# Costs in a list scheduler: durations by which the instructions of a transformer block are ordered, set to those of its trace

## The chip, the cores and the metric

The kernel runs on one core of a Trainium2 chip, in one launch. The metric is the device time of that launch in microseconds (us), as the median of several executions. The core's engines each work through an instruction list of their own: TensorE (PE, matrix products), VectorE (DVE), ScalarE (ACT), GpSimd (POOL) and SyncE (SP, which here only issues DMA transfers). Semaphores hold an instruction back until what it needs is there. The order inside each list is fixed when the program is built.

## The reference

One transformer block over an input x of 4 sequences of 1024 rows of 512 fp32 numbers. `c` makes six vectors per sequence; attention has 16 heads of 32 with one shared key and value head; the feed-forward part has Walsh-Hadamard transforms (`fwht`) before each of its two products (gate and up count as one). In the code below, cut and shortened, the first half is attention with its causal softmax and output projection, `gb` is clamped like `ga`, and `t` is the feed-forward part.

```python
mod = (_silu(c) @ wmod).reshape(4, 6, 1, -1)
sa, ca, ga, sb, cb, gb = (mod[:, n] for n in range(6))
ga = (2 * (ga >= 0) - 1) * jnp.maximum(jnp.abs(ga), 0.25)
h = _layernorm(x) * (1 + ca) + sa
x = x + ga * attention(h)
h = _layernorm(x) * (1 + cb) + sb
t = fwht(h * SU_ug) / 64
t = _silu(t @ W_gate.T * (Wscale_g * 64)) * (t @ W_up.T * (Wscale_u * 64))
t = fwht(t * SU_dp) / 64
x = x + gb * (t @ W_down.T * (Wscale_dp * 64))
```

## The kernel before

**Work.** The 4096 rows are 8 blocks of 512 rows, each of 4 tiles of 128 rows. A block goes through attention, tile by tile, and then through the feed-forward part (FFN) as a whole. The second transform and the scales are multiplied into the down weights once, in a preparation at the start (`butterflies` L965, `transforms` L986 and L989, copied by ACT at L992 and stored as wd_d). `mods` (L882, L886, L891, L932) makes the six vectors.

**Attention of a tile.** Score products (L503, PE), row minima of the negated scores (L527, DVE), exponentials with their sums (L550, ACT), reciprocals (L564, DVE), scaling (L584, ACT), transposes (L599, DVE), the product with the values (L627, PE, many small 32x32 products) and its copy out (L641, ACT). For the first block, products with a folding matrix (L684) and a copy (L687, ACT) bring the heads together; for the others an exchange through memory (o_d) and two additions on POOL (L664, L665). The output projection is called at L300, and its result is multiplied by `ga` on DVE (L701). POOL adds it to the residual (L716, L718), the sum is stored (x_d<-xr), and DVE makes its statistics (L305, L306), POOL the reciprocal deviation (`rstd_op`, L311 and L312).

**From attention to the FFN.** In the first three blocks DVE normalises (L316), PE transposes (L339), and products with a Hadamard matrix (L796), a copy (L801, ACT) and sums (L804, DVE) give the FFN's input `bt`. From the fourth block on (block 3, counted from 0) the generator `transformed` does it outside PE: two DVE operations normalise and modulate (L747, L749), 18 additions and subtractions of 256 columns on POOL make the transform (L755), DVE transposes in 32x32 squares (L758), four stores take a tile to memory (xTf_d<-xr) and two loads bring back half a block (bt<-xTf_d). In both forms four DVE subtractions (L808) then form T1 to T4.

**FFN.** The gate and up products of one of 16 chunks are one 2x2 product in Strassen's form, with seven products instead of eight (`gate_up`, all at L1078). POOL makes the four sums of weights (`mixes`, L1042), ACT copies partial results out (`copies`, L1152 and L1156), DVE adds them (`sums`, L1165), and `multiply` forms silu(gate) × up: tanh on ACT (L1181), a product for both halves of the rows (L1183, DVE), then g1 for the second half (L1186) and g0 for the first (L1191). `down` (L1216, PE) takes the first half of the rows while the chunks come, the second half later, with down weights in a ring of three buffers, loaded again for each half (wd<-wd_d). `outputs` multiplies by `gb` (L1245) and adds the residual (L1250). All transfers that SyncE issues stand at L289, in one order.

**What orders the work.** Nothing of this order is written by hand. Every step is a Python generator (a stream) that yields operations `Op(eng, cost, emit, reads, writes)`. `Flow` is a list scheduler that runs while the program is built. It keeps the time at which each engine becomes free and at which each buffer was written and read, by the operations' costs and not by the chip; for every stream's next operation it works out when that could begin, takes the earliest and all others of the same engine that begin within SLACK (0.3) of it, and emits the one of the lowest rank. Ranks stand in a list at the end of the kernel. The engines' lists are the order of emission. A result from another engine counts as there LATENCY (0.2) after its end; a change of PE's mode costs SWITCH (0.16); a transfer costs 3.9 per MB on one shared channel, and 1.5 to land. So a cost changes no instruction; it moves the point at which an operation is taken, and what is taken before it.

```python
some = [h for h in heads if h[2][2].eng == lead[2].eng and h[0] <= first + self.SLACK]
return min(some, key=lambda h: (h[2][0](), h[0]))
```

FFN weights are loaded and FFN products emitted only after a hand-over (stream `hand_over`), which waits for the preparation's last transform and `mods`.

Of the kernel before, what the change touches and what calls it, by code (L numbers as in the profile page):

```python
# [11 lines left out]
ALU = mybir.AluOpType  # L12
# [15 lines left out]
HB = 256  # L28
# [18 lines left out]
class Flow:  # L47
# [4 lines left out]
    LATENCY = 0.2  # L52
    SLACK = 0.3
    SWITCH = 0.16
    TRANSFER = 3.9

    def __init__(self):
# [10 lines left out]
    def ready(self, op):  # L68

        t = 0.0  # L70

        def after(found):
            if found is None:
                return 0.0
            at, eng = found
            return at if eng == op.eng else at + self.LATENCY

        for k in op.reads:
            if k not in self.wrote:
                return None  # L80
            t = max(t, after(self.wrote[k]))
        for k in op.writes:
            t = max(t, after(self.wrote.get(k)), after(self.read.get(k)))
        return t
# [76 lines left out]
def adaln_block(ctx, tc, x_d, small_d, const_d, wmod_d, qwT_d, kwT_d, vwT_d, vb_d, owT_d, ob_d,  # L161
# [147 lines left out]
    def rstd_op(dst, src, keys, key):  # L309
        def emit():  # L310
            nc.gpsimd.tensor_scalar_add(dst, src, EPS)  # L311
            nc.gpsimd.tensor_tensor(dst, dst, mhalf[:, 0:dst.shape[-1]], ALU.pow)  # L312
        return Op("POOL", 2.0, emit, keys, [key])

    def norm_op(x, xk, m, rs, rkey):
        return Op("DVE", 0.62, lambda: nc.vector.tensor_scalar(x, x, m, rs, ALU.subtract, ALU.mult), [rkey], [xk])  # L316
# [290 lines left out]
    def attend():  # L607


        while True:  # L610
            yield until(to_attend, "turns")
            if not to_attend:
                break
            u = to_attend.popleft()
            yield banks.have(4)
            bb = banks.take(4)
            w = u.heads * 32
            nkt = u.kmax // P
            pv = u.head(0, u.heads).rearrange("p (h k) -> p h k", k=u.kmax)

            def products():
                for kt in range(nkt):
                    v0 = u.kv[kt // NT] * (TB // 32) + kt % NT * 4
                    for g in range(4):
                        for c in range(4):
                            k = kt * P + 32 * c
                            nc.tensor.matmul(ps[rows[c], bb[g], 0:w], vrep[rows[g], v0 + c, :],  # L627
                                             pv[rows[g], :, k:k + 32],
                                             start=(kt == 0), stop=(kt == nkt - 1))
            yield Op("PE", nkt * (mm(w) + 0.22), products,  # L630
                     [u.key(h) for h in range(u.heads)] + [("vrep", j) for kb in range(u.t + 1) for j in u.half_keys(
                         kb, TB if kb < u.t else u.kmax - kb * TB)],
                     [bk(b) for b in bb] + [("through", u.k)], mode="tiles")
            st.attended += 1
            for h0 in range(0, u.heads, 8):
                half = (u.h0 + h0) // 8
                qn = 2 * (u.i * NT + u.ql) + half
                yield lambda: st.folded >= qn - 1
                o = oT[:, half].rearrange("p j (c g q) -> p g c j q", c=2, g=4)
                for g in range(4):  # L640
                    yield Op("ACT", act_cost(HB), lambda: nc.scalar.copy(  # L641
                        o[:, g], ps[:, bb[g], h0 * 32:h0 * 32 + HB].rearrange("p (c j q) -> p c j q", c=2, q=32)),
                        [bk(bb[g])], [("oT", half)])
                    if h0 + 8 == u.heads:
                        banks.give(bb[g])
                (to_finish if u.i < EXCHANGED else to_exchange).append((u.i, u.ql, half))
            if u.h0 + u.heads == H and u.ql == NT - 1:
                st.attended_blocks = u.i + 1
        over["attend"] = True

    def exchange():


        while True:
            yield until(to_exchange, "attend")
            if not to_exchange:
                break
            i, ql, half = to_exchange.popleft()
            o, key = oT[:, half], ("oT", half)
            yield load(0.5, o_d[half], o, [("o_d", half)], [key])  # L660
            for j, r in enumerate(rows):
                yield load(0.125, o[r], o_d[half].rearrange("(c d) j x -> j d c x", c=4)[j], [key], [("o_d", half)])
            o = o.rearrange("p c x -> p (c x)")
            yield Op("POOL", 1.3, lambda: nc.gpsimd.tensor_add(o[:, 0:512], o[:, 0:512], o[:, 512:1024]), [], [key])  # L664
            yield Op("POOL", 0.66, lambda: nc.gpsimd.tensor_add(  # L665
                aT[:, 2 * half:2 * half + 2, :].rearrange("p c q -> p (c q)"), o[:, 0:HB], o[:, HB:512]), [key], ["aT"])
            st.folded += 1
            to_finish.append((i, ql, half))
        over["exchange"] = True

    def finish():

        while True:
# [4 lines left out]
            if i < EXCHANGED:  # L678
                yield banks.have(1)
                bo, = banks.take(1)  # L680

                def folds():
                    for j, r in enumerate(rows):
                        nc.tensor.matmul(ps[r, bo, 0:HB], fold, oT[:, half, j, :], start=True, stop=True)  # L684
                yield Op("PE", 0.5, folds, [("oT", half)], [bk(bo)], mode="cols")
                st.folded += 1
                yield Op("ACT", act_cost(HB), lambda: nc.scalar.copy(  # L687
                    aT[:, 2 * half:2 * half + 2, :], ps[:, bo, 0:HB].rearrange("p (c q) -> p c q", c=2)), [bk(bo)], ["aT"])
                banks.give(bo)
            if half == 0:  # L690
# [42 lines left out]
    def transformed():  # L733


        for n in range(ROWS * NT, NBLK * NT):
# [3 lines left out]
            if n == ROWS * NT or n % NT == 0 and new_batch(i):  # L740
                yield lambda: st.normed >= ROWS
                for k, (dst, c) in enumerate(((sc2r, 0), (bi2r, 2))):
# [1 line left out]
                               [("gates", 3 + k)])  # L744
            yield lambda: bool(to_fwht)
            _, m, rs = to_fwht.popleft()
            yield Op("DVE", 0.7, lambda: nc.vector.scalar_tensor_tensor(x, x, m[:, 0:1], sc2r, ALU.subtract, ALU.mult),  # L747
                     [("v4", 0), ("mvf", j)], [xk])
            yield Op("DVE", 0.7, lambda: nc.vector.scalar_tensor_tensor(x, x, rs, bi2r, ALU.mult, ALU.add),  # L749
                     [("v4", 2), ("rstdf", j)], [xk])  # L750
            u, w = x, ht
            for _ in range(9):
# [9 lines left out]
    def second_norms():  # L762


        for i in range(NBLK):
            b = order[i][0]
            for hf in range(2):
# [30 lines left out]
                yield Op("PE", mm(HB, 4), products, [("v4", dc) for dc in range(NDC)] + ["had"],  # L798
                         [bk(b) for b in bb], mode="full")
                w2 = u2.rearrange("p a n -> p (a n)")  # L800
                yield Op("ACT", act_cost(512), lambda: nc.scalar.copy(w2, ps[:, bb[1], :]), [bk(bb[1])], ["u2"])  # L801
                banks.give(bb[1])
                for e, k in (("add", hf), ("sub", 2 + hf)):
                    yield Op("DVE", 0.7, lambda: getattr(nc.vector, "tensor_" + e)(  # L804
                        bt[:, k].rearrange("p a n -> p (a n)"), ps[:, bb[0], :], w2), [bk(bb[0]), "u2"], [("bt", k)])
                banks.give(bb[0])
            for o, u, w in ((T1, B12, B11), (T2, B22, T1), (T3, B22, B12), (T4, B21, T2)):
                yield Op("DVE", 0.7, lambda: nc.vector.tensor_sub(bt[:, o], bt[:, u], bt[:, w]),  # L808
                         [("bt", u), ("bt", w)], [("bt", o)])
            st.normed = i + 1  # L810

# [59 lines left out]
    def mods():  # L871
        for _ in range(6):
# [10 lines left out]
            yield Op("PE", mm(512), products, [("raw", s)], [bk(o)], mode="cols")  # L883
            busy[s] = False
            m = ym
            yield Op("ACT", act_cost(512), lambda: nc.scalar.copy(m, ps[:, o, :]), [bk(o)], ["ym"])  # L886
            pm = ps[:, o, 0:NDC * B].rearrange("p (a b) -> p a b", b=B)

            def summed():
# [145 lines left out]
    def mixes():  # L1035
        yield lambda: st.prepared
        for k in range(NW):
            a = weights(k)
            yield lambda: st.wg_loaded > k and st.wu_loaded > k and st.sums_used > k - 2
            for e, o, x, y in (("add", "S1", "A21", "A22"), ("sub", "S2", "S1", "A11"), ("sub", "S4", "A12", "S2"),  # L1040
                               ("sub", "S3", "A11", "A21")):
                yield Op("POOL", 0.66, lambda: getattr(nc.gpsimd, "tensor_" + e)(a[o][0], a[x][0], a[y][0]),  # L1042
                         [a[n][1] for n in (x, y) if n != "A21" or o != "S3"], [a[o][1]])
            st.mixed = k + 1

# [98 lines left out]
    def copies():  # L1144
        for n in range(2 * NW):
# [3 lines left out]
            bank = where[k]  # L1149
            if kind == "sp":  # L1150
                yield lambda: st.g1mul > k - 2
                yield Op("ACT", act_cost(512), lambda: nc.scalar.copy(  # L1152
                    s[:, 0:3:2, :], ps[:, bank, :].rearrange("p (a n) -> p a n", a=2)), [bk(bank)], [sk[0], sk[2]])
                st.sp = k + 1
            else:
                yield Op("ACT", act_cost(HB), lambda: nc.scalar.copy(s[:, 1, :], ps[:, bank, 0:HB]), [bk(bank)], [sk[1]])  # L1156
                to_sum.append(("g1", k))

    def sums():
# [15 lines left out]
    def multiply():  # L1175
        for k in range(NW):
# [3 lines left out]
            th, bank = ff["th"], where[k]  # L1180
            yield Op("ACT", act_cost(512), lambda: nc.scalar.activation(  # L1181
                th, s[:, 0:2, :], AF.Tanh, scale=wgh[:, f:f + 1]), [sk[0], sk[1]], ["th"])
            yield Op("DVE", 0.7, lambda: nc.vector.scalar_tensor_tensor(  # L1183
                th, th, 1.0, s[:, 0:2, :], ALU.add, ALU.mult), [sk[0], sk[1]], ["th"])
            yield lambda: st.v > k and st.downs1 > k - NFC
            yield Op("DVE", 0.46, lambda: nc.vector.scalar_tensor_tensor(  # L1186
                ff["g1"][:, f, :], th[:, 1, :], cg[:, f:f + 1], s[:, 2, :], ALU.mult, ALU.mult),
                [sk[2], "th"], [("g1", f)])
            st.g1mul = k + 1
# [128 lines left out]
```

## Time and profile before

| What | Before |
|---|---|
| Median of 3 executions (lowest, highest) | 2051.14 us (2047.05, 2052.68) |
| Profiled execution: its own time | 2046.4 us |
| Span in the profile | 2044.6 us |
| Mean granted TensorE clock | 0.989 |
| DMA traffic | 285.47 MB, mean 140 GB/s |
| L747, L749 (DVE), mean | 0.93, 0.95 us (0.75 where undisturbed) |
| L1183, L1186, L1191 (DVE), mean | 0.80, 0.66, 0.47 us |
| L808 (DVE), mean | 0.77 us |
| L1152, L1156 (ACT), mean | 0.59, 0.37 us |
| L641, L687 (ACT), mean | 0.38, 0.37 us |
| L801, L886 (ACT), mean | 0.59, 0.58 us |
| L1042 (POOL), mean of its four | 0.83, 0.77, 0.76, 0.75 us |
| L665 (POOL), mean | 0.77 us |
| L311 and L312 together (POOL), mean | 0.96 us (tile of the second norm) |
| L755 (POOL), mean | 0.64 us |

The profile shows one execution. "Busy" is the time in which an engine has an instruction under way; a row such as `L1078 PE MATMUL ps<-bt,wg` names line, engine, operation and tiles (written first). An idle time before an instruction is put down to what ended last before it ("<-DVE bt L808"), or to "issue" where the profile shows no such thing. Slices divide the span into 40 equal parts, and a digit gives tenths; PEclk is the TensorE clock that was granted, in tenths of full speed. The waits of an engine are listed with their total in us, their number and the longest.

### The profile page before, as it was taken

The numbers are of one execution on the slowest core, as the hardware profiler recorded it, in microseconds if no ns is written. First come the engines' busy times: TensorE is split into PE (matmuls) and PEld (weight loads), VectorE is DVE, ScalarE is ACT, GpSimd is POOL, SyncE is SP. The second block draws the span as 40 slices with busy tenths as digits, with TensorE's granted clock in tenths as the row PEclk, the third lists the DMA queues.
The fourth block names the chain that finished last, engine by engine and source line by source line (L and its number), as shares of the span: only waits on it lengthen the run. The fifth ranks groups of instructions, "written<-read, shape, count | busy, mean of one in ns | idle before, by whom it ended". The sixth has DMA issues, their size and how long they took to land.

```text
span 2044.6 us, 41680 instructions
## 1 busy us (share of the span) xinstructions
PE 1955.1 (96%) x15720; PEld 1264.7 (62%) x15720; DVE 1376.8 (67%) x3131; ACT 1133.5 (55%) x2391; POOL 973.5 (48%) x1246
## 2 busy tenths in 40 slices
PE   6997999999999999999999999998999999999998
PEld 4554666646676566655576566664566746675774
DVE  3885867777747567787748787766578877732441
ACT  3676766676557455666546665577356765510220
POOL 2662454414433576554545156534775535653441
PEclk9897999999999999999999999999999999999999
DMA  6424544454335755465344553357544355335333
GB/s 213 120 73 128 154 149 129 155 168 126 103 111 163 204 145 140 138 183 157 113 115 116 186 160 104 98 147 196 182 129 130 102 170 143 113 112 175 116 104 116
DMA packets 368464, 285.47 MB, mean 140 GB/s; under 512 B 112500, under 2 KB 300020, under 8 KB 368264
## 3 DMA queue, kind: packets, MB, share of 16 engines
q1 hardware_dynamic: 364328, 280.39, 47.0%
q10 hardware_dynamic: 3936, 2.43, 0.4%
q8 instruction: 124, 2.03, 0.4%
q14 instruction: 76, 0.62, 0.1%
HBM read 220.83 MB, written 61.91 MB: 138 GB/s over the span
## 4 chain that ended last, share of the span: by engine, by line
PE 85%; DVE 5%; DMA 5%; issue 2%; POOL 2%; SPq 1%; ACT 0%; POOLq 0%; ACTq 0%; DVEq 0%
PE ps L1078 36%; PE ps L1216 19%; PE ps L300 11%; PE ps L627 9%; PE ps L503 7%; DMA wd<-wd_d 1%; DMA raw<-in_wmod 1%; SPq L289 1%; DVE p L599 1%; DVE p L527 1%; PE ps L986 1%; PE ps L989 1%; DMA x_d<-xr 1%; DVE s L1165 1%; DVE g L1191 0%
## 5 line engine op out<-in xcount | busy, mean ns | idle before, releaser
L1216 PE MATMUL ps<-wd,g 128*128 128x512 f32 x1024 | 482.3, 605 | 27.4 <-DVE g L1191 16.7
L550 ACT ACTIVATE p<-p,nm 128x512 f32<-128x512 f32 (+7 forms) x512 | 391.2, 767 | 62.4 <-DVE nm L527 62.3
L1078 PE MATMUL ps<-bt,ws 128*128 128x256 f32 x1536 | 378.3, 382 | 2.8 <-DVE bt L808 1.9
L584 ACT ACTIVATE p<-p,rden 128x640 f32<-128x640 f32 (+7 forms) x480 | 348.0, 783 | 48.5 <-DVE rden L564 48.4
L599 DVE STREAM_TRANSPOSE p<-p 128x512 f32<-128x512 f32 (+7 forms) x256 | 342.7, 1358 | 42.3 <-ACT p L584 38.7
L1165 DVE TENSOR_TENSOR s<-ps,s 128x256 f32<-128x256 f32 x384 | 160.2, 420 | 298.1 <-PE ps L1078 227.5
L1216 PEld LDWEIGHTS ps<-wd,g 128*128 128x128 f32 x1024 | 185.6, 190 | 258.4 <-issue 189.9
L1078 PEld LDWEIGHTS ps<-bt,ws 128*128 128x128 f32 x1536 | 289.6, 191 | 58.8 <-issue 13.6
L527 DVE CUSTOM_DVE_ANT_0 p<-ps,maskw 128x512 f32<-128x512 f32 (+3 forms) x512 | 278.4, 583 | 69.2 <-PE ps L503 68.5
L1042 POOL TENSOR_TENSOR ws<-wu 128x256 f32<-128x256 f32 x128 | 105.8, 827 | 365.6 <-DMA wu<-in_wupT 309.2
L1078 PE MATMUL ps<-bt,wu 128*128 128x256 f32 x1024 | 269.0, 385 | 0.0
L1078 PE MATMUL ps<-bt,wg 128*128 128x256 f32 x1024 | 250.9, 381 | 0.4 <-DVE g L1191 0.3
L1078 PEld LDWEIGHTS ps<-bt,wu 128*128 128x128 f32 x1024 | 189.6, 190 | 83.0 <-issue 39.0
L1078 PEld LDWEIGHTS ps<-bt,wg 128*128 128x128 f32 x1024 | 192.8, 190 | 56.2 <-issue 24.3
L627 PE MATMUL ps<-p,vrep 32*32 32x256 f32 (+1 forms) x8256 | 196.8, 415 | 12.6 <-issue 8.2
L1181 ACT ACTIVATE th<-s,wgh 128x512 f32<-128x512 f32 x128 | 92.4, 722 | 183.3 <-DVE g L1191 128.1
L1156 ACT COPY s<-ps 128x256 f32<-128x256 f32 x128 | 47.7, 373 | 241.2 <-PE ps L1078 240.8
L503 PE MATMUL ps<-kT,qT 32*128 32x512 f32 (+3 forms) x1536 | 175.6, 530 | 1.5 <-DVE nm L527 1.4
L627 PEld LDWEIGHTS ps<-p,vrep 32*32 32x32 f32 x8256 | 121.4, 103 | 82.4 <-issue 35.9
L664 POOL TENSOR_TENSOR oT<-oT 128x512 f32<-128x512 f32 x56 | 73.4, 1311 | 170.6 <-DMA oT<-o_d 138.2
L1042 POOL TENSOR_TENSOR ws<-ws,wg 128x256 f32<-128x256 f32 x128 | 96.9, 757 | 112.0 <-DMA wg<-in_wgT 84.7
L641 ACT COPY oT<-ps 128x256 f32<-128x256 f32 x256 | 78.9, 384 | 106.7 <-PE ps L627 38.1
(119 smaller groups left out, 2382.9 us busy)
## 6 DMA issues: line engine op xcount, KB each, us to landing
wd<-wd_d SPq DMA_DIRECT2D x256, 256.0 KB, 2.8
wu<-in_wupT SPq DMA_DIRECT2D x128, 256.0 KB, 2.9
wg<-in_wgT SPq DMA_DIRECT2D x128, 256.0 KB, 3.5
o_d<-oT SPq DMA_DIRECT2D x56, 512.0 KB, 3.8
oT<-o_d SPq DMA_DIRECT2D x224, 128.0 KB, 3.4
xr<-in_x SPq DMA_DIRECT2D x32, 256.0 KB, 3.7
x_d<-xr SPq DMA_DIRECT2D x32, 256.0 KB, 2.1
xo<-x_d SPq DMA_DIRECT2D x32, 256.0 KB, 3.7
```

What stands on the lines that cost most here:

```text
L300: nc.tensor.matmul(out, l, r, start=(k == 0), stop=(k == len(pairs) - 1))
L503: nc.tensor.matmul(ps[:, bb[j], m * n:(m + 1) * n], qT[r, c, u.ql % 2 * P:(u.ql % 2 + 1) * P], kT[r, u.kv[kb] * TB:u.kv[kb] * TB + n], sta ...
L527: yield Op("DVE", 0.245 + 0.00103 * n, lambda: nc.vector.tensor_tensor_reduce(o, ps[:, bb[j], k * n:(k + 1) * n], m, -1.0, nm[:, slot, 0, ...
L550: yield Op("ACT", act_cost(u.kmax) + 0.19, lambda: nc.scalar.activation(e, e, AF.Exp, bias=nm[:, slot, u.t, j:j + 1], scale=-1.0, accum_ou ...
L584: yield Op("ACT", act_cost(u.kmax), lambda: nc.scalar.activation(e, e, AF.Copy, scale=r), [("rden", ds, c)], [u.key(h)])
L599: yield Op("DVE", 0.135 + 0.00105 * 2 * u.kmax, lambda: nc.vector.transpose(e, e), [], [u.key(h), u.key(h + 1)])
L627: nc.tensor.matmul(ps[rows[c], bb[g], 0:w], vrep[rows[g], v0 + c, :], pv[rows[g], :, k:k + 32], start=(kt == 0), stop=(kt == nkt - 1))
L1042: yield Op("POOL", 0.66, lambda: getattr(nc.gpsimd, "tensor_" + e)(a[o][0], a[x][0], a[y][0]), [a[n][1] for n in (x, y) if n != "A21" or o ...
L1078: nc.tensor.matmul(o, w[:, c, :], bt[:, t, c, :], start=start and c == 0, stop=stop and c == 1, skip_group_check=True)
L1165: yield Op("DVE", 0.43, lambda: nc.vector.tensor_add(s[:, j, :], ps[:, bank, half * HB:(half + 1) * HB], s[:, j, :]), [bk(bank)], [sk[j]])
L1181: yield Op("ACT", act_cost(512), lambda: nc.scalar.activation(th, s[:, 0:2, :], AF.Tanh, scale=wgh[:, f:f + 1]), [sk[0], sk[1]], ["th"])
L1216: nc.tensor.matmul(ps[:, acc[j], :], g[:, j * P:(j + 1) * P], ff["wd"][:, m % NWD, :], start=(f == 0), stop=(f == NFC - 1))
```

## The change

Only numbers by which `Flow` reckons are changed: 16 lines. A constant AFTER_PE of 0.15 is added to the time at which an operation on another engine may use a result of PE, on top of LATENCY. The cost of `rstd_op` goes from 2.0 to 1.0, those of six ACT copies from a formula (0.71 for 512 columns, 0.4975 for 256) to 0.586 and 0.384, and those of seven operations on DVE and POOL go up. No instruction, buffer, rank or rule is changed, and each engine has the same number of instructions of each kind as before; their order differs on all five engines. Behind L54 the changed kernel's line numbers are higher by one. Three places that repeat numbers are left out of the diff below: L687 (ACT copy, as L641), L749 (DVE, as L747) and L886 (ACT copy, as L801). L1191 keeps its 0.46.

```diff
 SWITCH = 0.16
+AFTER_PE = 0.15
...
-            return at if eng == op.eng else at + self.LATENCY
+            return at if eng == op.eng else at + self.LATENCY + (self.AFTER_PE if eng == "PE" else 0.0)
@@ -310 +311 @@ rstd_op
-        return Op("POOL", 2.0, emit, keys, [key])
+        return Op("POOL", 1.0, emit, keys, [key])
@@ -641 +642 @@ attend
-                    yield Op("ACT", act_cost(HB), lambda: nc.scalar.copy(
+                    yield Op("ACT", 0.384, lambda: nc.scalar.copy(
@@ -665 +666 @@ exchange
-            yield Op("POOL", 0.66, lambda: nc.gpsimd.tensor_add(
+            yield Op("POOL", 0.77, lambda: nc.gpsimd.tensor_add(
@@ -747 +748 @@ transformed
-            yield Op("DVE", 0.7, lambda: nc.vector.scalar_tensor_tensor(x, x, m[:, 0:1], sc2r, ALU.subtract, ALU.mult),
+            yield Op("DVE", 0.94, lambda: nc.vector.scalar_tensor_tensor(x, x, m[:, 0:1], sc2r, ALU.subtract, ALU.mult),
@@ -801 +802 @@ second_norms
-                yield Op("ACT", act_cost(512), lambda: nc.scalar.copy(w2, ps[:, bb[1], :]), [bk(bb[1])], ["u2"])
+                yield Op("ACT", 0.586, lambda: nc.scalar.copy(w2, ps[:, bb[1], :]), [bk(bb[1])], ["u2"])
@@ -808 +809 @@ second_norms
-                yield Op("DVE", 0.7, lambda: nc.vector.tensor_sub(bt[:, o], bt[:, u], bt[:, w]),
+                yield Op("DVE", 0.77, lambda: nc.vector.tensor_sub(bt[:, o], bt[:, u], bt[:, w]),
@@ -1042 +1043 @@ mixes
-                yield Op("POOL", 0.66, lambda: getattr(nc.gpsimd, "tensor_" + e)(a[o][0], a[x][0], a[y][0]),
+                yield Op("POOL", 0.78, lambda: getattr(nc.gpsimd, "tensor_" + e)(a[o][0], a[x][0], a[y][0]),
@@ -1152 +1153 @@ copies
-                yield Op("ACT", act_cost(512), lambda: nc.scalar.copy(
+                yield Op("ACT", 0.586, lambda: nc.scalar.copy(
-                yield Op("ACT", act_cost(HB), lambda: nc.scalar.copy(s[:, 1, :], ps[:, bank, 0:HB]), [bk(bank)], [sk[1]])
+                yield Op("ACT", 0.384, lambda: nc.scalar.copy(s[:, 1, :], ps[:, bank, 0:HB]), [bk(bank)], [sk[1]])
@@ -1183 +1184 @@ multiply
-            yield Op("DVE", 0.7, lambda: nc.vector.scalar_tensor_tensor(
+            yield Op("DVE", 0.8, lambda: nc.vector.scalar_tensor_tensor(
-            yield Op("DVE", 0.46, lambda: nc.vector.scalar_tensor_tensor(
+            yield Op("DVE", 0.66, lambda: nc.vector.scalar_tensor_tensor(
```

## Prediction, made before the changed kernel ran

> **What bounds the kernel now.** I read the profile's page first (engine shares, slices, chain), then the waits of TensorE, then the timeline around every wait over 2 us.
>
> ```profile
> PE 1955.1 (96%) x15720; PEld 1264.7 (62%) x15720; DVE 1376.8 (67%) x3131; ACT 1133.5 (55%) x2391; POOL 973.5 (48%) x1246
> ...
> PE   6997999999999999999999999998999999999998
> ...
> PEclk9897999999999999999999999999999999999999
> ...
> PE 85%; DVE 5%; DMA 5%; issue 2%; POOL 2%; SPq 1%; ACT 0%; POOLq 0%; ACTq 0%; DVEq 0%
> ```
>
> TensorE is busy for 1955.1 of 2044.6 us, and the other engines have slack. The change neither adds nor removes an instruction; it alters the order in which each engine gets them. So it can move only the 89.5 us in which PE idles, plus what PE loses at a lowered clock. By slices, 42 us of the idle time lie in the first 204 us and 47 behind. The waits of PE (us in total, times, longest) say what they are:
>
> ```profile
> PE ps L1216 <- DVE g L1191: 16.7, 23, 1.2
> ...
> PE ps L1216 <- DMA wd<-wd_d: 10.5, 7, 7.1
> ...
> PE ps L339 <- DVE xr L316: 7.8, 1, 7.8
> ```
>
> Two single waits of over 7 us and many of under 1.2. I laid the two instruction orders of PE side by side and gave each instruction the mean of its own row (0.446 us for a gate or up matmul, L1078; 0.858 for a down matmul, L1216; 0.043 for an attention matmul, L627; 1.07 for four score matmuls of 128x512, L503). Both orders then hold the same 1931 us of work, and each place has a position on that scale. Between "X can begin" and "PE needs X" I call the PE work the cover of X's chain; where the chain is longer, PE waits for the difference.
>
> **Start-up (a gain).** In before, block 0's second normalisation stalls PE:
>
> ```profile
> 184.19 1.75 PE L339 MATMUL ps<-ident,xr 128*128 128x128 f32 x7 [7.84 <-DVE xr L316]
> ...
> 194.21 1.10 PE L1078 MATMUL ps<-bt,ws 128*128 128x256 f32 x4 [1.88 <-DVE bt L808]
> 196.07 3.65 PE L1078 MATMUL ps<-bt,ws 128*128 128x256 f32 x8 [0.77 <-issue]
> ```
>
> L316 waits for the store of x2 (x_d<-xr), which SyncE issued at 178.03 behind five loads of gate and up weights. Between the output projection (L300) and L339 there is 3.5 us of work. In the new order there is 10.7, and no weight load stands ahead of the store, against some 8 us that the chain needs: the 7.84 go, and with them the slow clock behind (by stretches of 10 us from 170, busy time times missing clock: 5.33 × 0.22 + 5.51 × 0.47 + 7.02 × 0.17 = 5.0). What is late next is the hand-over to the FFN. It is opened after the last Hadamard product of the preparation (L989), at position 118.8 instead of 107.2, and the first gate product stands at 129.1 instead of 118.8. In before the weights' chain (store of wd_d, loads of gb, wu, wg) takes 12.5 to 16 us. In the new order two more loads of 256 KB (xo) stand ahead of wu: about 17, with some 11 us of work over it, so a new stall of about 6 and 1.7 at the slow clock. Gains (7.84 + 1.88 + 0.77 of waits and 5.0: 15.5) less costs (7.7) leave −7 to −8; I take −8. If the loads land early, −15; if ACT and DVE hold PE up, +5: between the third and the eighth attention group the new order has 37 us of PE work against 42 of DVE and 39 of ACT, where before has 52 against 50 and 46.
>
> **Waits on g (a gain).** The first down products wait for L1191, the last DVE step of a chunk: 16.7 us. The higher costs of L1183, L1186 and the new term after PE let the scheduler put more work between. Products with under 1.5 us of cover behind the chunk's last gate product: 27 in before (9 with about 0, 6 with 0.5, 12 with 1.0), 15 in the new order (3, 8, 4). Where before waits 16.7/23 = 0.7 each, twelve fewer and smaller ones give −5 (−8 to −2). Mode changes of PE fall from 427 to 412: −1.
>
> **The two boundaries (a loss).** From block 3 on, a block's FFN input is made by a long chain outside PE. The DVE timeline of block 5 (counted from 0), in before; the start and the duration come first:
>
> ```profile
> 1398.16 0.69 DVE L701 TENSOR_TENSOR y<-ps,ga 128x512 f32<-128x512 f32 x1
> ...
> 1402.81 0.75 DVE L747 SCALAR_TENSOR_TENSOR xr<-xr,mvf,v 128x512 f32<-128x512 f32 x1
> 1403.67 0.75 DVE L749 SCALAR_TENSOR_TENSOR xr<-xr,rstdf,v 128x512 f32<-128x512 f32 x1
> ...
> 1421.08 0.71 DVE L758 STREAM_TRANSPOSE xr<-u 128x512 f32<-128x512 f32 x1 [1.05 <-POOL u L755]
> ...
> 1433.58 3.64 DVE L808 TENSOR_TENSOR bt<-bt 128x512 f32<-128x512 f32 x4 [5.97 <-DMA bt<-xTf_d]
> ```
>
> From the output projection's result (L701) to the first sum of the next input (L808) are 35.4 us, 36.3 with that sum; block 6 needs 32.4 the same way (1623.53 to 1655.92). Its parts: 6.3 to the first butterfly on POOL; 18 butterflies, 16.5 here, 11.0 at 0.612 each if nothing stands between; L758 0.7; four stores, 5 from L758 to the last landing; two loads, 7.3; a sum, 0.8. With nothing between (stores 2.0 to issue and 2.0 to land, loads 0.8 and 4.8, the medians of the DMA table) it is 6.3 + 11.0 + 0.7 + 4.0 + 5.6 + 0.8 = 28.4, an estimate from these rows, below which it hardly goes. The cover from L701 to the first gate product in before: 73, 65, 34, 30, 43 us for blocks 3 to 7. In the new order: 60, 22.9, 22.8, 66, 54. So blocks 4 and 5 both get some 23 us of cover for a chain of 28.4 to 36.3. At 33 PE waits about 10 in each; at the ends 5.5 and 13.4. Before has one such place, where PE in fact waits for a wd load queued behind these stores:
>
> ```profile
> 1432.35 3.37 PE L1216 MATMUL ps<-wd,g 128*128 128x512 f32 x4 [7.13 <-DMA wd<-wd_d]
> ```
>
> Its 7.13 and 1.4 of slow clock (3.37 against 1.98 for the same four) go, with up to 2 at block 6 (cover 30 for a chain of 32.4). The clock bears on this twice. This trace: behind the 7.84 us wait PEclk fell to 0.53 in the stretch 180 to 190 us and 0.83 in the next; behind 1.88 and 0.77 alone eight L1078 took 3.65 instead of 1.89. The Trainium skill (TensorE: Matmul & The Clock Gate, "Part 1: The HAM clock gate") says that an idle window of about 3.4 us halves the clock and one busy window restores it, windows running free; so a 10 us stall would cost half a window, 1.7, and a stall of 2.7 nothing. The rows show 1.4 to 5 for one long stall, and a charge after a short one: I take 2 each (by the rule the sum would be 0.6 lower). Sum: before's loss here is 7.13 + 1.4 and up to 2 at block 6, about 10; 2 × (10 + 2) − 10 = +14. Range: 2 × (5.5 + 1.4) − 10.5 = +3 to 2 × (13.4 + 2) − 8.5 = +22.
>
> **What is left.** Two wd loads stand behind 11 other transfers in SyncE's queue with 3.6 us of cover (before: one behind 8, counted above): 0 to 7 each, nearest row the 0.58 that a normal late wd load costs, so +2. From position 1278 to 1354 the new order has attention alone: 76 us of PE work against about 71 of ACT and 63 of DVE, so small waits come through; +5 (0 to +8). POOL's and DVE's other moves have cost nothing that I can find: they lie beside PE work of several us.
>
> **Sum:** −8 − 5 − 1 + 14 + 2 + 5 = +7 us. The profiled execution took 2046.4 (span 2044.6 and 1.8 around it), 4.7 under the median of 2051.14; a difference carries over: 2051.14 + 7 = 2058, or 2053 for an execution as quick as the profiled one.
>
> **The rivals.** The measurement of this kernel can tell about 0.3%, 6 us, from no change.
> - Slower, the forecast: 2058; with the boundaries at 13 each, 2066; with the start-up gain lost, 2071. Chance 0.47. For it: a chain with a floor of 28 us cannot hide behind 23 us of PE work, and 96% of the time a wait of PE is a wait of the kernel.
> - No change, 2051: the start-up gains its 14 (the weights land early), boundaries cost 12 net: −14 − 5 − 1 + 12 + 2 + 5 = −1. Chance 0.23. For it: the start-up sum has the widest bounds; against it: 2 more transfers really stand ahead of wu.
> - Faster, 2038: one mechanism, at the two boundaries. The 22.9 us of cover are work, not time: if the attention that stands there runs slower than its work by 2 us (its ACT and DVE are nearly as full as PE), and POOL has little else to do, so that the chain comes near its floor, 28.4 − 24.9 leaves 3.5 each with no clock lost. That replaces the 10 of before: 2 × 3.5 − 10 = −3; the crowding is then what hides the stalls, once 3 instead of 2 + 5; and −8 − 5 − 1 − 3 + 3 = −14. It decides from a chain of about 29 down. Chance 0.30. Against it: the two chains measured in before are 32.4 and 36.3, and POOL works for the next block in them too (L716, L664 and L665 took 3.3 us between the butterflies, and 1.5 went in a wait for xr<-in_x).
> - That the numbers don't reach the order is ruled out: the orders of all engines differ.
>
> Low end: the faster case, 2038 (with the start-up at −15 as well 2031, given up). High end: 2066 and 2071 as above, both together 2079; 2075 leaves about 1 in 10 out. Some 2 in 10 lie outside in all.
>
> **What would show it.** Right: the waits of L339 on L316 (7.8) are gone; L1216 on DVE g falls from 16.7 to about 11; two new PE idle stretches of about 10 us, ahead of the first L1078 of blocks 4 and 5 (about 1150 to 1200 and 1440 to 1490 us of the span), released by DVE bt L808 or DMA bt<-xTf_d, each with PEclk below 1; a wait of about 6 ahead of the first L1078 of all. Wrong: no PE idle over 5 us behind 250 us; chains from L701 to L808 of 29 us or less; or new waits of PE on ACT p L584 and DVE p L599 that add up to more than the boundaries.

## The result, and the profile after

The changed kernel took 2080.53 us (median of 4 runs, 2076.66 to 2082.97) against 2049.44 of the kernel before (4 runs, 2047.05 to 2052.68): ratio 1.0143, 95% interval 1.0125 to 1.0161. The sign was forecast, the size was not: +7 us stood in the prediction, +31 by the medians came, beyond the end of the range. The profiled execution took 2082.9, its span is 2081.0 against 2044.6: 36.4 longer. Line numbers of the changed kernel are higher by one, so its L301 is L300 of before. The page's lines:

```profile
PE 1976.4 (95%) x15720; PEld 1274.2 (61%) x15720; DVE 1381.7 (66%) x3131; ACT 1132.0 (54%) x2391; POOL 971.4 (47%) x1246
...
PE   6988999999999999999999799997899999999998
```

The first slices look much as before. Two new dips stand in the slices from 1145 to 1197 us (7) and from 1405 to 1509 (7, 8). The waits of PE in the changed kernel:

```profile
PE ps L628 <- DVE p L600: 24.8, 4, 10.8
PE ps L628 <- issue: 17.2, 17, 2.5
...
PE ps L1217 <- DVE g L1192: 7.5, 11, 0.9
...
PE ps L1217 <- DMA wd<-wd_d: 3.1, 5, 0.8
```

The waits for g fell from 16.7 to 7.5, those for wd from 10.5 to 3.1, and L340's on L317 for xr from 7.8 to 2.1. What came instead is the first line: attention products (L628) that wait for the transposes on DVE (L600), 4.2 us before. The second line was 8.2 before; the profile shows no cause for these waits. The two largest waits lie where the prediction had put its two stalls, ahead of the first gate products (L1079) of blocks 4 and 5. Block 4, PE's timeline:

```profile
1159.97 0.73 PE L504 MATMUL ps<-kT,qT 32*128 32x128 f32 x16
1171.48 4.85 PE L628 MATMUL ps<-p,vrep 32*32 32x256 f32 x160 [10.78 <-DVE p L600]
1176.25 1.14 PE L504 MATMUL ps<-kT,qT 32*128 32x512 f32 x8
1177.32 1.13 PE L1079 MATMUL ps<-bt,wg 128*128 128x256 f32 x4
```

and DVE's over the same stretch, where the FFN input's chain can be read from L702 to L809:

```profile
1141.74 0.69 DVE L702 TENSOR_TENSOR y<-ps,ga 128x512 f32<-128x512 f32 x1 [0.98 <-PE ps L301]
...
1168.46 2.87 DVE L600 STREAM_TRANSPOSE p<-p 128x1280 f32<-128x1280 f32 x2
1174.93 2.62 DVE L809 TENSOR_TENSOR bt<-bt 128x512 f32<-128x512 f32 x4 [3.60 <-DMA bt<-xTf_d]
```

L628 became ready at 1171.5, T1 (the first quarter of L809) at about 1175.6. So two chains end within some 4 us: attention's, which the record names, and the input's, which would have held PE next. Block 5:

```profile
1458.01 4.00 PE L628 MATMUL ps<-p,vrep 32*32 32x512 f32 x64 [9.96 <-DVE p L600]
1461.93 1.14 PE L504 MATMUL ps<-kT,qT 32*128 32x512 f32 x8
1463.85 3.31 PE L504 MATMUL ps<-kT,qT 32*128 32x512 f32 x6 [0.77 <-DVE nm L528]
1469.25 2.07 PE L504 MATMUL ps<-kT,qT 32*128 32x512 f32 x2 [2.09 <-DVE nm L528]
1471.86 5.46 PE L301 MATMUL ps<-ow,aT 128*128 128x512 f32 x8 [0.54 <-DVE nm L528]
```

Here the stall has a tail. The row at 1461.93 holds four score products (two records each) that run side by side. Behind it four such products ran one after the other, each released, by its time, by a row minimum on DVE:

```profile
1463.71 0.68 DVE L528 CUSTOM_DVE_ANT_0 p<-ps,maskw 128x512 f32<-128x512 f32 x1
...
1464.41 0.66 DVE L528 CUSTOM_DVE_ANT_0 p<-ps,maskw 128x512 f32<-128x512 f32 x1
...
1468.53 0.65 DVE L528 CUSTOM_DVE_ANT_0 p<-ps,maskw 128x512 f32<-128x512 f32 x1
```

They started at 1463.85, 1464.46, 1465.13 and 1469.25, each some 0.07 us after a minimum had ended. L301 then took 5.46 for what takes 3.60 at full clock. The clock went to half twice (each row: stretch, length, busy time of PE, PEld, DVE, ACT and POOL, then PEclk, DMA share, GB/s):

```profile
1451.57:1461.79 10.22, 3.78 (x64) 1.10 (x64) 8.18 (x20) 8.33 (x24) 8.06 (x12) 0.50 0.41 117
1461.81:1465.20 3.39, 2.62 (x28) 0.97 (x13) 1.98 (x7) 3.06 (x10) 3.23 (x6) 1.00 0.00 0
1465.22:1475.44 10.22, 7.59 (x10) 2.41 (x10) 7.51 (x17) 6.80 (x19) 5.41 (x9) 0.50 0.53 109
```

Busy time times missing clock is 1.9 + 3.8 = 5.7 us. Summed so by stretches of 10 us over the whole span, the slow clock costs 15.9 us before and 24.7 after.

**A ledger.** For every kernel: the start of a block's first gate product in the trace, less the PE work that stands before it in the list (row means, as in the prediction, whose matmul is two records of the trace), is PE's lag; its growth is time lost. Growth between a block's last and the next one's first gate or up product is the loss at that boundary. In us:

| Kernel | lag at first gate product | from there to block 3's last | boundary 4 | block 4 | boundary 5 | rest |
|---|---|---|---|---|---|---|
| before | 70.6 | 16.3 | 2.2 | 7.5 | 10.7 | 8.8 |
| changed | 71.5 | 20.6 | 16.7 | 5.2 | 28.7 | 9.8 |

Of the 36 us, 32.5 came at the two boundaries (14.5 and 18.0), 4.3 in blocks 0 to 3, 0.9 at the start. A boundary ends here with the first gate product, which needs none of T1 to T4; a wait for L809 can also fall just behind it.

### The profile page after: what moved, and what is told of

It is laid out like the page before. It is cut to its first block, busy times and chain, and to the rows that moved or that the text cites. A ratio compares the mean times of both kernels' runs of the same rounds, so it can differ in the third digit from the quotient of the medians.

```text
span 2081.0 us, 41689 instructions
## 1 busy us (share of the span) xinstructions
PE 1976.4 (95%) x15720; PEld 1274.2 (61%) x15720; DVE 1381.7 (66%) x3131; ACT 1132.0 (54%) x2391; POOL 971.4 (47%) x1246
## 4 chain that ended last, share of the span: by engine, by line
PE 83%; DVE 4%; POOL 4%; DMA 3%; issue 3%; ACT 1%; SPq 1%; POOLq 0%; ACTq 0%; DVEq 0%
PE ps L1079 36%; PE ps L1217 19%; PE ps L301 11%; PE ps L628 8%; PE ps L504 7%; DVE p L600 1%; DMA raw<-in_wmod 1%; POOL u L756 1%; SPq L290 1%; DVE p L528 1%; POOL xr L756 1%; DMA xr<-in_x 1%; DMA wd<-wd_d 0%; PE ps L797 0%; POOL p L582 0%
## 5 line engine op out<-in xcount | busy, mean ns | idle before, releaser
L1217 PE MATMUL ps<-wd,g 128*128 128x512 f32 x1024 | 482.3, 604 | 10.7 <-DVE g L1192 7.5
L1079 PE MATMUL ps<-bt,ws 128*128 128x256 f32 x1536 | 379.1, 383 | 2.5 <-ACT s L1153 2.5
L600 DVE STREAM_TRANSPOSE p<-p 128x512 f32<-128x512 f32 (+7 forms) x256 | 342.6, 1357 | 50.3 <-ACT p L585 47.1
L585 ACT ACTIVATE p<-p,rden 128x640 f32<-128x640 f32 (+7 forms) x480 | 347.4, 783 | 45.1 <-DVE rden L565 44.7
L1079 PEld LDWEIGHTS ps<-bt,ws 128*128 128x128 f32 x1536 | 289.0, 191 | 63.5 <-issue 10.0
L528 DVE CUSTOM_DVE_ANT_0 p<-ps,maskw 128x512 f32<-128x512 f32 (+3 forms) x512 | 277.7, 580 | 69.1 <-PE ps L504 68.9
L1079 PE MATMUL ps<-bt,wu 128*128 128x256 f32 x1024 | 268.5, 385 | 2.1 <-DVE s L1166 1.6
L1079 PE MATMUL ps<-bt,wg 128*128 128x256 f32 x1024 | 252.7, 383 | 1.1 <-DVE s L1166 1.0
L1079 PEld LDWEIGHTS ps<-bt,wu 128*128 128x128 f32 x1024 | 189.9, 190 | 85.2 <-issue 45.9
L628 PE MATMUL ps<-p,vrep 32*32 32x256 f32 (+1 forms) x8256 | 200.7, 419 | 42.6 <-DVE p L600 24.8
L1079 PEld LDWEIGHTS ps<-bt,wg 128*128 128x128 f32 x1024 | 193.8, 191 | 55.1 <-issue 22.1
L628 PEld LDWEIGHTS ps<-p,vrep 32*32 32x32 f32 x8256 | 121.2, 104 | 118.1 <-issue 60.5
L504 PE MATMUL ps<-kT,qT 32*128 32x512 f32 (+3 forms) x1536 | 186.4, 536 | 3.8 <-DVE nm L528 3.5
L665 POOL TENSOR_TENSOR oT<-oT 128x512 f32<-128x512 f32 x56 | 73.2, 1307 | 180.9 <-DMA oT<-o_d 119.5
L642 ACT COPY oT<-ps 128x256 f32<-128x256 f32 x256 | 77.8, 386 | 118.0 <-issue 38.8
```

The lines of the kernel that those rows point to most:

```text
L504: nc.tensor.matmul(ps[:, bb[j], m * n:(m + 1) * n], qT[r, c, u.ql % 2 * P:(u.ql % 2 + 1) * P], kT[r, u.kv[kb] * TB:u.kv[kb] * TB + n], sta ...
L528: yield Op("DVE", 0.245 + 0.00103 * n, lambda: nc.vector.tensor_tensor_reduce(o, ps[:, bb[j], k * n:(k + 1) * n], m, -1.0, nm[:, slot, 0, ...
L585: yield Op("ACT", act_cost(u.kmax), lambda: nc.scalar.activation(e, e, AF.Copy, scale=r), [("rden", ds, c)], [u.key(h)])
L600: yield Op("DVE", 0.135 + 0.00105 * 2 * u.kmax, lambda: nc.vector.transpose(e, e), [], [u.key(h), u.key(h + 1)])
L1079: nc.tensor.matmul(o, w[:, c, :], bt[:, t, c, :], start=start and c == 0, stop=stop and c == 1, skip_group_check=True)
L1217: nc.tensor.matmul(ps[:, acc[j], :], g[:, j * P:(j + 1) * P], ff["wd"][:, m % NWD, :], start=(f == 0), stop=(f == NFC - 1))
```

## The experiments

**Which chain holds PE at the boundaries.** Three kernels keep every list of the changed kernel and leave work out.

```diff
-                    yield Op("POOL", 0.66, lambda: getattr(nc.gpsimd, "tensor_" + fn)(
+                    yield Op("POOL", 0.66, lambda: (_ == 0 or n not in (19, 23)) and getattr(nc.gpsimd, "tensor_" + fn)(
```

> The changed kernel with the same orders, but of the last tile of blocks 4 and 5 only the first of the nine butterfly stages is computed: 16 of 18 POOL operations of each are left out, some 10 us of the chain from L702 to L809. Theory A (the two boundary stalls are the wait for the FFN input): both shrink by 8 to 10, the time falls from 2080.5 to about 2062. Theory B (PE waits there for attention, behind ACT and DVE): no change, 2078 to 2081. Theory C (both chains end within some 4 us of each other): at most 2 us at block 4 and some 5 at block 5, about 2075.

```diff
-                    yield Op("ACT", act_cost(u.kmax), lambda: nc.scalar.activation(
+                    yield Op("ACT", act_cost(u.kmax), lambda: 4 * u.i + u.ql in LIGHT or nc.scalar.activation(
...
-            yield Op("DVE", 0.135 + 0.00105 * 2 * u.kmax, lambda: nc.vector.transpose(e, e),
+            yield Op("DVE", 0.135 + 0.00105 * 2 * u.kmax, lambda: 4 * u.i + u.ql in LIGHT or nc.vector.transpose(e, e),
```

> The changed kernel with the same orders, but the scaling (L585, ACT) and the transposes (L600, DVE) of five attention tiles are left out, those that are under way at the two boundaries (tiles 20, 21, 25, 26, 27, counted from 0). Theory A: no change at the boundaries, 2076 to 2081. Theory B: the stalls of 10.8 and 10.0 go, about 2058. Theory C: only some 2 us at block 4 and a few at block 5, about 2074, and the wait of PE moves from DVE p L600 to DVE bt L809 or DMA bt<-xTf_d.

> Both cuts together, same orders. Theory A: as the short transform alone, about 2062. Theory B: as the light attention alone, about 2058. Theory C: far more than the sum of the two, about 2050, since only here both chains are shorter than PE's work.

Ratios to before: 1.0106 (1.0075 to 1.0138), 1.0137 (1.0099 to 1.0175) and 1.0077 (1.0049 to 1.0106), beside the changed kernel's 1.0143. The losses at the two boundaries, what the first 28 matmul records of the block behind it lose in addition (about one chunk), and the time from the start of L702 to the start of L809:

| Kernel | boundary 4 | next 28 | L702 to L809 | boundary 5 | next 28 | L702 to L809 |
|---|---|---|---|---|---|---|
| changed | 16.7 | 0.5 | 33.2 | 28.7 | 3.9 | 44.7 |
| short transform | 14.5 | 0.1 | 32.2 | 26.1 | 2.2 | 43.0 |
| light attention | 9.3 | 6.9 | 33.9 | 27.8 | 0.9 | 44.2 |
| both | 7.0 | 7.6 | 33.0 | 20.2 | 0.8 | 36.3 |

At block 4 none of the cuts brings more than 2.6 us (16.7 + 0.5 against 7.0 + 7.6): what light attention saves ahead of the first gate product is lost right behind it, where PE waits for the input. The short transform did not shorten the input's chain there. In the run with both cuts POOL is done at 1152.1, but the transpose L759 starts 9.8 us later:

```profile
1150.73 1.37 POOL L756 TENSOR_TENSOR u<-xr 128x256 f32<-128x256 f32 x2
...
1161.32 0.69 DVE L1246 TENSOR_TENSOR y<-ps,gb 128x512 f32<-128x512 f32 x1
1161.92 0.70 DVE L759 STREAM_TRANSPOSE xr<-u 128x512 f32<-128x512 f32 x1
...
1175.32 2.08 PE L1079 MATMUL ps<-bt,ws 128*128 128x256 f32 x4 [4.10 <-DVE bt L809]
```

L759 stands in DVE's list behind minima and an output (L1246), which need PE's results themselves. So at block 4 these runs tell less than they were meant to: in none is the input's chain shorter than 32 us. With light attention the loss stays at 16.2, now in waits for the copies L642 (2.3) and for the input (4.3) and at half clock behind them. What a shorter chain would bring was not run. At block 5 each cut alone brings 4 us, both together 11.6 with the 28 records (28.7 + 3.9 against 20.2 + 0.8), which is theory C's pattern; the chain is 8 us shorter there, yet PE waits for L809 in none of these runs at block 5. Theory C's sizes were too large: in time both together bring 0.66%, some 13 us where 30 were expected. The light attention's trace shows what takes over. Block 4, PE:

```profile
1168.35 2.07 PE L1079 MATMUL ps<-bt,ws 128*128 128x256 f32 x4 [4.32 <-DVE bt L809]
```

Block 5, DVE:

```profile
1458.30 0.71 DVE L759 STREAM_TRANSPOSE xr<-u 128x512 f32<-128x512 f32 x1 [6.80 <-POOL u L756]
```

and PE:

```profile
1459.65 2.07 PE L504 MATMUL ps<-kT,qT 32*128 32x512 f32 x2 [6.03 <-DVE nm L528]
```

At block 4 it is the chain of the prediction, 4.3 us. At block 5 that chain acts by way of DVE's queue: DVE stands 6.8 us before L759, waiting for POOL's butterflies, and the minima (L528) that free the banks of the score products stand behind it.

The same cuts, everywhere:

```diff
-(_ == 0 or n not in (19, 23))
+(_ == 0 or n < 12)
...
-LIGHT = (20, 21, 25, 26, 27)
+LIGHT = range(16, 32)
```

> The changed kernel with the same orders, but without the scaling (L585) and the transposes (L600) in all attention tiles from the 17th on, and without the last eight butterfly stages in all of blocks 3 to 7. If PE loses time in the gaps because ACT, DVE and POOL set the pace there, the 16.7 us at block 4 and 28.7 at block 5 fall below 4 and 10, and the time to about 2035. If PE's own order, SyncE's queue or the clock set it, they stay above 10 and 20, and the time above 2060.

Ratio 1.0072 (1.0051 to 1.0093). Boundary 4: 7.0 and 10.0 more in the next 28 records, boundary 5: 20.3 and 1.0. At block 4 the first number lies between the two sides, but with the 28 records nothing came off (17.0 against 17.2; L702 to L809 takes 33.1). At block 5 and in time (median 2067.5) the result lies on the rival's side, though a third of block 5's loss went. In the gap at block 5 (1350 to 1473 us) PE still idles 9.7 us and loses 4.3 to the clock:

```profile
PE ps L504 <- DVE nm L528: 4.4, 2, 3.1
PE ps L628 <- issue: 2.3, 3, 1.1
PE ps L628 <- ACT p L551: 2.1, 1, 2.1
PE ps L301 <- DVE nm L528: 0.8, 1, 0.8
```

The minima (L528) lead this list; the score products there are also recorded busy some 5 us longer than by their row means. ACT waits 3.2 us in front of L642 for POOL (L666), and the exponentials behind it wait too. POOL in the changed kernel suggested why:

```profile
1446.28 0.57 POOL L313 TENSOR_TENSOR rstdf<-rstdf,mhalf 128x1 f32<-128x1 f32 x1
1453.33 1.26 POOL L717 TENSOR_TENSOR xr<-xr,obga 128x512 f32<-128x512 f32 x1 [6.49 <-DMA xr<-in_x]
1454.56 1.18 POOL L756 TENSOR_TENSOR u<-xr 128x256 f32<-128x256 f32 x2
```

L717, an addition for the next block, waits for its load while the butterflies (L756), ready at 1450.4, stand behind it. Two runs leave L717 out at the two boundaries:

```diff
-                yield Op("POOL", 1.3, lambda: nc.gpsimd.tensor_add(x, x, obga), ["obga"], [xk])
+                yield Op("POOL", 1.3, lambda: n in (20, 24) or nc.gpsimd.tensor_add(x, x, obga), ["obga"], [xk])
```

> The changed kernel with the same orders, but POOL's addition L717 is left out for two tiles (20 and 24), those that stand in POOL's list between L750 and the butterflies at the two boundaries. In the changed kernel it waited there 2.96 and 6.49 us for the load xr<-in_x, with the butterflies behind it: they began 2.4 and 4.1 us after L750's end. If this wait is part of the two losses: 2 us off at block 4 and 4 to 6 at block 5, 2073 to 2075. If attention sets the pace there anyway: below 2 us in all, 2078 to 2081.

> The run with light attention and short transforms everywhere, and these two L717 left out too. There L717 still waited 5.97 us at block 5, and L665, L666, the copies L642, the exponentials and the minima stood behind it one after the other. If that queue is what holds block 5's loss at 20.3 us: it falls to about 13, and the time from 2067.5 to about 2060. If not: 2065 to 2069.

Ratios 1.0126 (1.0101 to 1.0150) and 1.0088 (1.0061 to 1.0114). In the first, the boundaries lose 14.3 and 26.4: 2.4 and 2.3 less, a small part (2.8 and 3.7 with the next 28 records). In the second 7.0 and 21.8: nothing. POOL's wait in front of L717 is not what keeps the 20 us at block 5.

**Which of the numbers does it.** Hunks of the change, as shown with it, each put into the kernel before (the fifth kernel: all of them but L747 and L749). AFTER_PE is written as a number in place:

```diff
-            return at if eng == op.eng else at + self.LATENCY
+            return at if eng == op.eng else at + self.LATENCY + (0.15 if eng == "PE" else 0.0)
```

> The kernel before with AFTER_PE alone. Cover from L701 to the first gate product: 31 us at block 4, 22 at block 5, over 34 elsewhere from block 3 on. Cover theory: block 5 loses about 20 us as in the changed kernel, block 4 some 4, waits of down products for g fall to about 6: with before's 8.5 at block 5 given back about 2051 + 20 + 4 - 8.5 - 10 = 2056. If AFTER_PE is what does the whole damage: 2075 or more.

> The kernel before with the costs of L1183 and L1186 alone. Cover 39 us at block 4, 25 at block 5. Cover theory: block 5 loses about 15 instead of 8.5, waits for g stay near 17 (15 products of no cover at all instead of 9): about 2058. If these costs are what brings the gain at g: 2045.

> The kernel before with the six ACT copy costs alone. Cover 67 us at block 4, 36 at block 5, 73 at block 7. Cover theory: no loss at block 4, block 5 as before (about 8) or less, waits for g about 18: 2047 to 2052. It has the late hand-over of the changed kernel (last L989 at position 125 instead of 114), so its lag at the first gate product shows what the start-up of the changed kernel is worth alone: -8 by the prediction, about +1 by the changed kernel's trace.

> The kernel before with one number of the change only: the cost of the four subtractions T1 to T4 (L808) 0.77 instead of 0.70. The order that comes out has 146, 106, 79, 150 and 73 us of PE work between L701 and the first gate product of blocks 3 to 7. Cover theory: no boundary stall at all, so faster than before by its 7.1 and the slow clock behind it, about 2040; the waits of the down products for g stay at 17 or rise a little (28 products of under 1.5 us cover). Rival (any change of an order that was tuned costs, or PE waits for attention anywhere): 2050 or more.

> The changed kernel with only L747 and L749 put back to 0.70. Cover 63 us at block 4, 28 at block 5. Cover theory: block 4's loss of some 14 goes, block 5's falls to about 10 (28 of cover for a chain of 33 to 36), waits for g stay near 8: about 2080 - 14 - 12 = 2054. If the loss comes from the denser attention everywhere and not from these two places: 2070 or more.

All were slower than before, and by 16 to 38 us slower than my theory expected; the table below has the ratios. AFTER_PE alone lowers the waits for g to 11.8 us; the costs of L1183 and L1186 alone, to which I had put that gain down too, raise them to 26.8. The six ACT copies, whose new numbers lie within 0.02 us of their rows, do most harm alone. One number moved by 0.07 us, L808's, costs 0.3%. Of the parts run alone none is the culprit, and these four sum to far more than the whole. L747, L1042, L665 and `rstd_op` were not run alone.

The ACT-copies run was also to price the late hand-over: its first gate product comes with a lag of about 3 us more than before's, so no gain of 8 shows there either.

Laying the losses of these seven kernels beside their lists gave another rule than mine. Call gap the PE work that stands between the last gate or up product of one block and the first of the next. Over the 35 boundaries of blocks 3 to 7 the loss is 0.27 × gap − 1.9 us, correlation 0.94: in a gap PE has only attention and the rest of the down products. (With the next 28 records counted in, it is 0.27 × gap − 0.2, correlation 0.91.) This is a fit to results already seen, not a shown cause. Four new orders were picked by their gaps before they ran; they are hunks of the change again, the first of them AFTER_PE with this one:

```diff
-        return Op("POOL", 2.0, emit, keys, [key])
+        return Op("POOL", 1.0, emit, keys, [key])
```

> Kernel before with two of the changes: AFTER_PE and the cost of rstd_op (alone, AFTER_PE cost 1.2%). Gap theory: what PE loses at a boundary follows the PE work that its list holds between the last gate or up product of one block and the first of the next (the gap): over 35 boundaries of the seven orders run so far (blocks 3 to 7) the loss is 0.27 x gap - 1.9 us, correlation 0.94. This order has gaps of 18, 8, 66, 14 and 2 us at blocks 3 to 7, 107 in all against 105 in before: the same 19 us at the boundaries (16 of them at block 5), and fewer waits for g (10.6 us of missing cover against 24.5): 2042 to 2050. Rival (each new number costs about 1%, and costs add up): 2075 or more.

> Kernel before with L747 and L749 at 0.94 and L808 at 0.77. Gaps of 7, 13, 42, 26 and 7 us, 95 in all against 105; missing cover for g 19.3 against 24.5. Gap theory: 0 to 2, 2, 9, 5, 0 at the boundaries, 16 in all; 2044 to 2050. Rival (costs add up: 0.3% for L808 alone and more for L747): 2060 or more.

> As the run with L747, L749 and L808, and rstd_op at 1.0 too. Its order has the longest gaps of all that were built: 58, 54, 95, 50 and 7 us, 266 in all. Gap theory: 14, 13, 24, 12 and 0 us at the boundaries, 62 in all against before's 19: about 2090, the slowest of all. Rival (it is AFTER_PE or the FFN costs that slow the changed kernel, neither of which is here): 2050 to 2065.

> The kernel before with L747 and L749 at 0.94, L808 at 0.77 and 0.09 after PE: of some 90 orders built from parts of the change, one of the three with the shortest gaps and good cover (14, 10, 62, 14, 2 us at blocks 3 to 7, 102 in all; missing cover for g 15.6 us against before's 24.5). Gap theory: as before at the boundaries, 4 to 5 us less behind g: 2044 to 2050, a version that beats both if the rest stays equal. If the losses within the FFN stretches change with every order by as much as the gaps do: 2050 to 2065.

| Order (numbers of the change that it has) | sum of gaps, blocks 3 to 7 | loss in them | ratio to before (95%) |
|---|---|---|---|
| before (none) | 105 | 16.4 | 1 |
| AFTER_PE | 136 | 26.6 | 1.0118 (1.0095 to 1.0141) |
| L1183, L1186 | 122 | 23.4 | 1.0141 (1.0114 to 1.0168) |
| ACT copies | 152 | 41.7 | 1.0185 (1.0170 to 1.0200) |
| L808 | 167 | 27.6 | 1.0031 (1.0018 to 1.0044) |
| all but L747, L749 | 212 | 41.3 | 1.0109 (1.0082 to 1.0137) |
| all (the changed kernel) | 216 | 53.5 | 1.0143 (1.0125 to 1.0161) |
| AFTER_PE, rstd_op | 107 | 27.8 | 1.0032 (1.0009 to 1.0056) |
| L747, L749, L808 | 95 | 5.7 | 0.9995 (0.9982 to 1.0009) |
| the same with rstd_op | 266 | 42.2 | 1.0122 (1.0105 to 1.0139) |
| L747, L749, L808, 0.09 after PE | 102 | 18.7 | 0.9969 (0.9954 to 0.9983) |

In time one of the four came out as forecast: the last, with the ratio 0.9969. AFTER_PE with `rstd_op` took 2059.2 where at most 2050 was forecast, the order with the longest gaps 2074.9 where 2090 was, and the third order 2051.0, 1 us over its range. The new 20 boundaries give a correlation of 0.80 and miss the line by 3.7 us on average; it asked for too much in the order with rstd_op (62 against 42). The loss can also move: with L747, L749 and L808 boundary 5 lost 1.1 us at a gap of 42, but block 5 itself 16.3 instead of 4.8, over half of it in the first 28 records. Over whole orders the gap sums correlate with the time by only 0.59; the line through them misses the order of the ACT copies by 22 us. So the rule sorts boundaries, and times only roughly.

The last row, at 2039.58 against 2046.38 in that call, is faster than both kernels. Its gaps promised no gain and gave none; its waits for g are 7.3 us instead of 16.7. Its lag at the first gate product is also some 9 us lower than before's, and from there to the end of block 3 it loses some 12 more, so what makes it faster is not shown.

## Why the prediction was right in sign and wrong in size

The sign came from the boundaries, as forecast. The step that failed is the boundary term: it let the 23 us of PE work beside the input's chain count as work that runs freely (+14), and the two boundaries cost +32.5. The start-up term (−8) failed too: +0.9 was measured.

- **Waits on g:** right in direction and a little small (−9.2 of waits where −5 stood). The reason was half wrong: AFTER_PE lowers them by itself, the costs of L1183 and L1186 by themselves raise them. The ledger shows none of this gain: outside the start and the two boundaries the changed kernel loses 3.0 us more than before, so some 12 us of other losses came there. The waits put down to "issue" (17.2 against 8.2) are part of them; no run separates them.
- **Start-up, −8: failed.** The wait of 7.84 went, and no stall of 6 at the hand-over came; yet the lag at the first gate product is 71.5 against 70.6. Seven kernels with the changed start give 67.5 to 71.5, four with the old one 68.3 to 70.9, so the order is worth about −1 there (means 69.3 and 70.0). From 70 us to the first gate product the listed waits of PE are 17.6 against 19.3 us: L628 on L600 (4.0), L301 on L528 (2.9) and others stepped in, and from 170 to 203 us the clock averaged 0.83. DVE is busy for 70.2 of the 80 us from 70 to 150 before, for 71.1 after. The term "15.5 of waits and clock go" took each wait as its own. That ACT and DVE hold PE up, the term's far bound, fits these waits, but no run tested it. The prediction's "two single waits of over 7 us" also left one out: L339 waits 11.3 us for L316 (xn) at the start of the kernel, 9.3 after, which the change hardly touched.
- **Boundaries, +14: mis-sized, +32.5.** The two stalls came in the places named, 10.8 and 10.0 for "about 10 in each", but that the lengths agree is in part luck: neither was released by L808 or by bt<-xTf_d, both by the transposes (L600 after, L599 before), and waits on these, 24.8 against 4.2, were on the prediction's own list of signs of being wrong. At block 4, where 12 of the 23 us are down products and the rest attention, the input's chain is the mechanism too: with light attention PE waits for L809, and the loss stays. At block 5 all of the cover is attention, it waits for ACT and DVE itself, and PE never waits for L809. What followed the stall there was not in the sum: score products and L301 waiting for minima (3.4 us), and score products running one at a time. The clock took 5.7 us there instead of 2, because it fell twice. Of the Trainium skill's rule (TensorE: Matmul & The Clock Gate, "Part 1: The HAM clock gate") the way up holds: both times the clock came back after 3.4 us in which PE was busy throughout (L628 from 1458.01, L301 from 1471.86). The way down does not: the rule asks for an idle window of about 3.4 us, and the second fall came after 3.39 us in which PE was busy for 2.62. So the rule's nothing for a short stall, which the prediction set beside its own charge, is too low here.
- **wd loads, +2: did not come.** Apart from the 7.13, which the boundary term had, these waits went from 3.4 to 3.1. The 11 transfers ahead of the two loads cost at most 0.8 us.
- **What is left, +5:** its 76 us (position 1278 to 1354) end at block 5's first gate product, so the ledger books what came there with the boundary. That blocks 0 to 3 (4.3), block 4 (−2.3) and the rest (1.0) sum to 3.0 is no confirmation.
- **The rivals.** The faster case needed a chain of under 29 us; it took 33.2 at block 4 and 44.7 at block 5 (L702 to L809). The slower end of 2066 to 2071 had longer stalls and a lost start-up gain, not the tail.

What stays open: why boundary 5 loses 20 us even with light attention, short transforms and no L717. The exponentials, the minima and the exchange through memory, which those runs kept, are the candidates; the waits name the minima first, but leaving them out was not tried. At block 4 an order with L759 ahead of L1246 was not tried.

## What to carry to other kernels

In a list scheduler that is close to the bound, truer durations need not give a better order. Here one cost changed by 0.07 us reshuffles what follows, and parts of such a change don't add up (+1.2, +1.4, +1.9, +0.3% alone, +1.4% together with the rest). Look first at the stretches in which the bound engine has only work that others pace; such work is a poor cover. Where one long wait was removed in a stretch whose second engine was nearly 90% busy, the waits regrouped. And when work is left out to shorten a chain, measure the chain: ten us less on POOL shortened the chain by 1 us at most at block 4, because the next link stood in DVE's list behind work that waited for PE.

## What was not expected of the hardware

- One order's start differs from run to run: over seven kernels with the same lists to that point, the lag at the first gate product spans 67.5 to 71.5 us.
- Score products that are released one by one keep PE busy for longer: at block 5 six records of L504 took 3.31 us, partly at half clock, where eight take 1.14. PE's busy time rose by 21.3 us with the same instructions, 10.8 of them in L504's group (175.6 to 186.4), so the busy share (96 and 95%) hides much of the loss.
- The clock fell to half twice within 24 us, for 10.2 us each: after a stall of 10 us, and again after 3.39 us at full clock in which PE was busy for 2.62.
